# A four-layer graph network on one core: the first transposed adjacency made on TensorE, two of four turn transfers issued by ScalarE, and the last element's third layer in plain products

## The chip, the cores and the metric

The kernel runs on one core of one Trainium2 chip. The metric is device time in microseconds (us), as the median of several executions of the whole program. One more execution is recorded by the profiler; its trace and its page are what this document reads. The profiled execution has a time of its own, which stands in the table below beside its span (first to last instruction).

## What is computed

There are 32 independent batch elements. Each has 512 nodes of 128 features (`x`) and a dense 512x512 matrix `adj`. Four residual layers run one after the other on each element; every layer first normalizes its rows and applies ReLU. Cut to what matters:

```python
h = relu(layernorm(x)); A1 = adj + I; r = rowsum(A1) ** -0.5
x = x + leaky_relu((A1 * r[:, None] * r[None, :]) @ (h @ W) + b)               # layer 0

h = relu(layernorm(x))
i, o, n = (elu(h @ Wk.T + bk) for Wk, bk in (in, out, node))
x = x + tanh(concat([adj @ i, n, adj.T @ o]) @ W_upd.T + b_upd)                # layer 1

f = relu(layernorm(x)); R = adj / rownorm(adj); C = adj / colnorm(adj)
for k in range(4):       # inputs of 128, 128, 256, 384 features: earlier f are appended
    f = tanh(concat([R @ (f @ ws + bs), f @ wn + bn, C.T @ (f @ wd + bd)]) @ wu + bu)
x = x + f                                                                      # layer 2

h = relu(layernorm(x)); m = tanh(adj @ (h @ W_msg.T + b_msg))
x = x + GRU(m, h)                                                              # layer 3
```

All of it is float32.

## The kernel before, in words

**Tiles.** A node dimension of 512 is cut into `NC = 4` chunks of 128 partitions. An element holds `a` (its `adj`, 1 MB) and `aT` (the transposed `adj`), each as 128 x 4 x 512 in SBUF. Layer 3 loads the transposed matrix a second time (`aT2`), since layer 2 has changed `aT` in place.

**Products.** TensorE works in two halves of 64 output rows: `by_halves` issues one matmul for each half, and the two run side by side. In this document a *pair* is such a product on both halves. Each of its two matmuls leaves two records in the trace, so a pair is four records.

**Layer 2 with fewer products.** `features` (steps 1, 3 and 4 of layer 2) and `edges` (step 2) do the products with the two matrices in a scheme of seven products of half size instead of eight. It needs sums of blocks: `made_of` makes them of `aT` and `a` on VectorE (four operations of 128x512 for each matrix), `left_sums` makes them of the features, and the results are put together by more additions on VectorE (`p`, `de`, `to`, line 792).

**Turns.** Features are needed both with nodes on partitions and with features on partitions. For elements 2 to 30, `turned` does the change: VectorE transposes 32x32 blocks into `blk` (line 698), four DMAs write `blk` to DRAM (`away`, line 707: `turn_turned<-blk`), and one DMA reads it back (line 711: `turned<-turn_turned`). All five are issued by SyncE (SP), which issues nearly all DMAs. An element has seven turns (three in `transposed`, one in `second`, three in `added_rows`), 203 in all. Elements 0, 1 and 31 (`at_ends`) turn on TensorE instead (`turn_on_pe`: a product with the identity).

**Order.** `Plan` collects every operation of all 32 elements as an `Op` with an engine, an estimated duration, what it reads and writes, and a key: the element's due time (`PERIOD`) less the longest way from the operation to the element's end, plus a hand-set shift by the name of the result (`LATER`). `order` then plays the engines forward with these estimates, takes the ready operation of the lowest key on each engine, gives it its buffers (`places`: 27 of 2 KB, 7 of 4 KB and so on, and the 8 banks of PSUM), and so fixes the order of each engine's instructions. On the chip each engine goes through its list in that order. Loads of later elements are held back while a turn is under way (`yields`, `way`). The loads in `FIRST` go out ahead of everything else, in the order of that list. `kept_warm` puts products of no use (`ps_idle<-ident`) on TensorE wherever the plan has it idle for longer than its constant `SHORT`.

**Start.** Element 0 is on its own: `x0`, `a0` and `aT0` are loaded in pieces of 256 KB, `normed_by_chunk` sums the rows of each piece of `a` on VectorE and takes a power on GpSimd, the diagonal blocks of `aT` get the identity added (`diag`, line 1023), and the first aggregation `psh` (lines 1024 to 1031) runs through `aT` column chunk by column chunk. Then come `lin` (line 1038) and the rest of layer 0, beside the folding of the weights (`fold`, `foldb`, in `setup`), which reads `raw0`, `raw2` and `raw3`.

**End.** Element 31 has nobody behind it: its last layer is `gates_turned`, whose parts are worked off in halves.

Of the kernel before, what the change touches and what calls it, by code (L numbers as in the profile page):

```python
# [14 lines left out]
AF = mybir.ActivationFunctionType  # L15
# [3 lines left out]
P = 128  # L19
# [6 lines left out]
ENDING = -5.5  # L26
LATER = {"de": 4, "nb": 4, "rows": 1, "ps_a2": -4, "f3": -4, "s34": 2, "n": 4, "sd": -10, "w": 2, "st2": -8, "f4": 2, "blk": 1, "rep": 1, "s12": 4, "ps_second": -1, "hn": -2, "f2p": 4, "f2": 2, "ps_gate": -1}
SMALL = 8

FIRST = ["x0", "a0", "aT0", "c", "raw0", "w1", "r1", "raw2", "raw3", "x1", "a1", "aT1", "x2", "a2", "aT2"]  # L30

# [260 lines left out]
def gnn_stack(  # L292
# [15 lines left out]
    dram = ctx.enter_context(tc.tile_pool(name="dram", bufs=1, space=bass.MemoryType.DRAM))  # L308
    plan = Plan(sb, psum, {"bank": 8, "s2": 27, "s4": 7, "s6": 4, "s8": 8}, {"bank": 0, "s2": 2, "s4": 0, "s6": 0, "s8": 0})

# [161 lines left out]
    def program(b):  # L472
# [144 lines left out]
        def load(dst, src, kb, rank, behind=()):  # L617

            name = f"{rank}{b}"
            rank, kb = first(name), kb * (2 if name == "a0" else 1)  # L620

            n = NC // pieces
            for k in range(pieces):
                s = slice(k * n, (k + 1) * n)
                op("SP", 0.4, lambda s=s: nc.sync.dma_start(dst.ap()[:, s, :], src[:, s, :]),
                   [], [(dst, set(range(NC)[s]))], kb=kb / pieces, rank=rank, yields=rank is None, behind=behind)

        op("SP", 0.4, lambda: nc.sync.dma_start(xt.ap(), x[b]), [], [xt], kb=256, rank=first(f"x{b}"), yields=f"x{b}" not in FIRST)
        load(a, adj[b], 1024, "a")
        load(aT, adjt[b], 1024, "aT")  # L630

# [62 lines left out]
        def turned(m, name, quiet=False):  # L694
# [8 lines left out]

            def away(k):
                if bounce.tile is None:
                    bounce.tile = dram.tile([P, NC, P], F32, name=bounce.name, tag=f"{bounce.kind}_{bounce.slot}", bufs=1)
                nc.sync.dma_start(bounce.tile[:, k, :].rearrange("(b s) n -> s b n", b=NC), blk.ap()[k * P // NC:(k + 1) * P // NC])  # L707

            for k in range(NC):
                op("SP", 0.4, lambda k=k: away(k), [blk], [(bounce, {k})], kb=64)  # L710
            back = op("SP", 0.4, lambda: nc.sync.dma_start(mT.ap(), bounce.tile), [bounce], [mT], kb=256)
# [130 lines left out]
        def features(i, sd, nodes, made, f_new):  # L842

            st = buf("s4", (P, 4, NC, Q), "st")
            left_sums(H, lambda h, k: lambda: sd.ap().rearrange("p (q k) (o h f) -> p q k o h f", k=2, o=2, h=2)[:, :, k, :, h, :],
# [60 lines left out]
        def edges(f1r, made, ge):  # L908


            st = buf("s2", (P, 4, 2, Q), "st2")
# [109 lines left out]
        else:  # L1021
            for k in range(NC):
                op("DVE", t_tt(P), lambda k=k: nc.vector.tensor_tensor(diag.ap()[:, k:k + 1, :], *own(k, 1), op=ALU.add), [(aT, {k}), ID], [(diag, {k})])
        psh = plan.bank("agg")
        for c in range(NC if b == 0 else 0):
            for lo, hi in ((0, c * P), (c * P, (c + 1) * P), ((c + 1) * P, N)):
                if lo == hi:
                    continue
                mm(psh, lambda t, lo=lo, hi=hi: t[:, lo:hi], lambda c=c: hr.ap()[:, c, :],
                   (lambda c=c: diag.ap()[:, c, :]) if lo == c * P else (lambda c=c, lo=lo, hi=hi: aT.ap()[:, c, lo:hi]),  # L1030
                   hi - lo, c == 0 and lo == 0, c == NC - 1 and hi == N, [(hr, {c}), (diag if lo == c * P else aT, {c})])
        if b:
# [87 lines left out]

        made = [made_of(m) for m in (aT, a)]
        for i, (wsd, wn) in enumerate(W_L2):
# [100 lines left out]
```

## Time and profile before

| | |
|---|---|
| median of 4 runs | 2253.42 us (2250.16 to 2254.67) |
| the profiled execution | 2251.52 us |
| its span | 2249.7 us |
| TensorE (PE) busy | 2231.9 us, 99% |
| VectorE (DVE) busy | 1762.9 us, 78% |
| ScalarE (ACT) busy | 1219.0 us, 54% |
| GpSimd (POOL) busy | 230.9 us, 10% |
| DMA | 264.43 MB, mean 118 GB/s |
| granted TensorE clock | 1.0 over the whole span |

Between the profiled time and the span lie 1.8 us, and the median lies 1.9 us above the profiled time. "Busy" counts an instruction from its start to its end; matmuls overlap, so a busy TensorE can still have small holes. The products of no use count as busy too. SPq and ACTq are the instruction queues of SP and ScalarE when they issue DMAs. L838 and L364 are the lines of the two helpers that issue nearly all products, L792 the one that issues VectorE's sums, so groups are told apart by their tiles.

### The profile page before, as it was taken

Reading aid. Unit: us, or ns where it says so; the run is one execution under the profiler, and the core shown is the slowest. Engines: PE = TensorE matmul, PEld = TensorE weight load, DVE = VectorE, ACT = ScalarE, POOL = GpSimd, SP = SyncE. Lnnn points to the kernel's source line nnn. Section 1 sums busy time; section 2 is a strip of 40 time slices with the busy share of each in tenths; the row PEclk is TensorE's granted clock in tenths of the full one; section 3 lists DMA queues with packets and bytes.
Section 4 is the critical chain, followed back from the end, with each engine's and each line's share of the span. In section 5 each row is a group of like instructions: output and inputs, shape, how many; then the busy total and the mean of one; then the engine's idle time right before and its main releaser. Section 6 shows DMA issues by size and latency. Waiting matters only on the chain.

```text
span 2249.7 us, 47725 instructions
## 1 busy us (share of the span) xinstructions
PE 2231.9 (99%) x18332; PEld 1437.7 (64%) x18332; DVE 1762.9 (78%) x4657; ACT 1219.0 (54%) x2793; POOL 230.9 (10%) x203
## 2 busy tenths in 40 slices
PE   9999999999999999999999999999999999999999
PEld 6665566676556656775567755666666655655576
DVE  7776878888778788788788787887787887787754
ACT  8654565654556545556545556545565455564323
POOL 2110111100111101111001111011111011110000
PEclk9999999999999999999999999999999999999999
DMA  7131434344344444344443344443444443433211
GB/s 257 39 103 42 140 109 128 118 138 133 107 126 129 123 132 122 107 126 118 140 132 112 121 127 122 136 124 109 133 124 127 136 120 109 128 106 114 76 53 57
DMA packets 199139, 264.43 MB, mean 118 GB/s; under 512 B 25984, under 2 KB 130688, under 8 KB 198912
## 3 DMA queue, kind: packets, MB, share of 16 engines
q1 hardware_dynamic: 198624, 261.26, 38.2%
q8 instruction: 144, 2.36, 0.4%
q14 instruction: 83, 0.68, 0.1%
q10 hardware_dynamic: 288, 0.13, 0.0%
HBM read 199.18 MB, written 62.13 MB: 116 GB/s over the span
## 4 chain that ended last, share of the span: by engine, by line
PE 84%; DVE 6%; DMA 5%; SPq 2%; ACT 1%; issue 1%; POOL 0%; POOLq 0%; DVEq 0%; ACTq 0%
PE ps_pa L838 17%; PE ps_agg L364 16%; PE ps_cd L838 16%; PE ps_sd L364 10%; PE ps_seven L364 4%; PE ps_pb L838 3%; DMA turned<-turn_turned 3%; PE ps_b L838 3%; PE ps_gate L364 2%; PE ps_upd L364 2%; PE ps_second L364 2%; PE ps_a L838 2%; SPq L707 2%; PE ps_c L838 1%; PE ps_msg L364 1%; DMA turn_turned<-blk 1%
## 5 line engine op out<-in xcount | busy, mean ns | idle before, releaser
L838 PE MATMUL ps_pb<-made,st 128*64 128x256 f32 x1536 | 392.8, 379 | 0.0
L677 POOL TENSOR_TENSOR sc<-v,neg_half 128x4 f32<-128x4 f32 x127 | 171.3, 1349 | 1762.6 <-DVE v L638 1717.8
L364 PE MATMUL ps_sd<-w_sb,f 128*64 128x256 f32 x2048 | 267.4, 379 | 0.5 <-ACT f L1127 0.4
L838 PE MATMUL ps_pa<-aT,sd 128*64 128x256 f32 x768 | 227.9, 379 | 0.0
L838 PE MATMUL ps_cd<-aT,st 128*64 128x256 f32 x768 | 223.1, 380 | 2.3 <-DVE st L792 2.0
L838 PE MATMUL ps_cd<-a,st 128*64 128x256 f32 x768 | 223.8, 379 | 0.0
L838 PE MATMUL ps_pa<-a,sd 128*64 128x256 f32 x768 | 223.7, 379 | 0.0
L838 PEld LDWEIGHTS ps_pb<-made,st 128*64 128x64 f32 x1536 | 209.4, 137 | 0.8 <-DVE p L792 0.4
L364 PEld LDWEIGHTS ps_sd<-w_sb,f 128*64 128x64 f32 x2048 | 163.1, 137 | 69.0 <-issue 18.4
L838 PE MATMUL ps_pb<-made,sd 128*64 128x256 f32 x768 | 197.0, 379 | 0.0
L901 ACT ACTIVATE f<-to,cf_sb 64x512 f32<-64x512 f32 x192 | 117.5, 612 | 125.5 <-DVE to L792 121.0
L689 ACT ACTIVATE h<-xr,nb,sc 128x128 f32<-128x128 f32 x384 | 158.0, 484 | 25.0 <-DVE nb L685 24.6
L778 DVE TENSOR_TENSOR sd<-ps_sd,rf_sb 128x512 f32<-128x512 f32 x192 | 123.1, 683 | 45.7 <-PE ps_sd L364 45.6
L838 PEld LDWEIGHTS ps_pa<-aT,sd 128*64 128x64 f32 x768 | 105.1, 137 | 65.3 <-issue 25.3
L792 DVE TENSOR_TENSOR p<-p,ps_pb 64x256 f32<-64x256 f32 x192 | 81.4, 424 | 64.8 <-PE ps_pb L838 41.9
L838 PEld LDWEIGHTS ps_pa<-a,sd 128*64 128x64 f32 x768 | 105.1, 137 | 41.1 <-issue 2.2
L364 PE MATMUL ps_agg<-a,rep 128*64 128x512 f32 x512 | 128.2, 592 | 0.0
L364 PE MATMUL ps_agg<-aT,msg 128*64 128x512 f32 (+1 forms) x528 | 126.6, 579 | 0.0
L792 DVE TENSOR_TENSOR to<-p,ps_pb 64x256 f32<-64x256 f32 x96 | 40.8, 425 | 107.1 <-PE ps_pb L838 105.9
L838 PEld LDWEIGHTS ps_cd<-aT,st 128*64 128x64 f32 x768 | 102.4, 137 | 34.2 <-issue 4.6
L364 PE MATMUL ps_agg<-aT,rep 128*64 128x512 f32 x512 | 122.9, 592 | 0.1
L838 PEld LDWEIGHTS ps_cd<-a,st 128*64 128x64 f32 x768 | 104.4, 137 | 27.9 <-issue 1.1
(224 smaller groups left out, 5828.9 us busy)
## 6 DMA issues: line engine op xcount, KB each, us to landing
aT<-in_adjt SPq DMA_DIRECT2D x124, 512.0 KB, 6.1
turn_turned<-blk SPq DMA_DIRECT2D x696, 64.0 KB, 1.8
turned<-turn_turned SPq DMA_DIRECT2D x174, 256.0 KB, 2.8
a<-in_adj SPq DMA_DIRECT2D x62, 512.0 KB, 7.3
rows<-bounce SPq DMA_DIRECT2D x32, 512.0 KB, 4.1
shares<-bounce SPq DMA_DIRECT2D x32, 512.0 KB, 3.7
x<-in_x SPq DMA_DIRECT2D x32, 256.0 KB, 4.5
out<-xr SPq DMA_DIRECT2D x31, 256.0 KB, 2.7
```

The lines of the kernel that those rows point to most:

```text
L364: nc.tensor.matmul(to[c], weight[:, c], data, start=start, stop=stop, skip_group_check=True)
L677: op("POOL", t_pow(n), lambda: nc.gpsimd.tensor_tensor(inv.ap()[:, :n], v8.ap()[:, :n], neg_half[:, :n], op=ALU.pow), [v8, NH], [(inv, {0})])
L689: op("ACT", t_act(D, 2), lambda c=c: nc.scalar.activation(h.ap()[:, c, :], xin.ap()[:, c, :], AF.Relu, bias=nb.ap()[:, c:c + 1], scale=inv ...
L707: nc.sync.dma_start(bounce.tile[:, k, :].rearrange("(b s) n -> s b n", b=NC), blk.ap()[k * P // NC:(k + 1) * P // NC])
L778: op("DVE", t_tt(N), lambda ps=ps, h=h: nc.vector.tensor_add(sd.ap()[:, 2 * h:2 * h + 2, :], ps.ap().rearrange("p (j v) -> p j v", j=2), a ...
L792: return op(engine, us, lambda: eng.tensor_tensor(o(), x(), y(), op=ALU.subtract if sign < 0 else ALU.add), reads, writes)
L838: nc.tensor.matmul(to(), lhs(), rhs(), start=start, stop=True, skip_group_check=True)
L901: op("ACT", t_act(n, 1), lambda: nc.scalar.activation(f_new.ap()[rows, cols], src(), AF.Tanh, bias=cf_sb[rows, i:i + 1]), reads + [(CF, {i ...
```

## The change

Six edits, made together:

1. **First transpose.** `aT0` is no longer loaded. TensorE turns each of the four row chunks of `a0` into a bank of PSUM (16 pairs of 128 columns), ScalarE copies each bank into `aT`, and `diag` is added out of PSUM. The first aggregation goes by rows of `a` instead of columns: block by block as the row chunks come.
2. **Turns.** The second and fourth of the four transfers of a turn (`k % 2`) are issued by ScalarE (`nc.scalar.dma_start`) as an operation in ScalarE's list. The read back stays with SP.
3. **Last element.** With `PLAIN = 1` element 31 makes no block sums: `features` and `edges` take plain products of 512 columns, gathered in one bank (`made is None`).
4. **Buffers.** 29 places of 2 KB instead of 27 (and 3 kept free for older elements instead of 2), 6 of 4 KB instead of 7.
5. **Keys.** `LATER` has six more names.
6. **Estimate of a load.** The plan takes the load of `a0` as 1.2 times its size and not 2 times.

The diff, cut to its core:

```diff
-LATER = {"de": 4, ..., "f2": 2, "ps_gate": -1}
+PLAIN = 1
+LATER = {"de": 4, ..., "f2": 2, "ps_gate": -1, "node": -8, "y": 8, "made": -1, "f1r": 4, "turn_turned": -1, "ge": 4}
...
-FIRST = ["x0", "a0", "aT0", "c", "raw0", "w1", "r1", "raw2", "raw3", "x1", "a1", "aT1", "x2", "a2", "aT2"]
+FIRST = ["x0", "a0", "c", "raw0", "w1", "r1", "raw2", "raw3", "x1", "a1", "aT1", "x2", "a2", "aT2"]
...
-    plan = Plan(sb, psum, {"bank": 8, "s2": 27, "s4": 7, "s6": 4, "s8": 8}, {"bank": 0, "s2": 2, "s4": 0, "s6": 0, "s8": 0})
+    plan = Plan(sb, psum, {"bank": 8, "s2": 29, "s4": 6, "s6": 4, "s8": 8}, {"bank": 0, "s2": 3, "s4": 0, "s6": 0, "s8": 0})
...
-            rank, kb = first(name), kb * (2 if name == "a0" else 1)
+            rank, kb = first(name), kb * (1.2 if name == "a0" else 1)
...
-        load(aT, adjt[b], 1024, "aT")
+        if b:
+            load(aT, adjt[b], 1024, "aT")
+        else:
+            turned_rows = [plan.bank(f"turn_{r}") for r in range(NC)]
+            for r, ps in enumerate(turned_rows):
+                for c in range(NC):
+                    turn_on_pe(ps, c, lambda r=r, c=c: a.ap()[:, r, c * P:(c + 1) * P], [(a, {r})])
+                op("ACT", t_act(N), lambda r=r, ps=ps: nc.scalar.copy(
+                    aT.ap()[:, :, r * P:(r + 1) * P], ps.ap().rearrange("p (c n) -> p c n", c=NC)), [ps], [(aT, {0, 1, 2, 3, NC + r})])
...
-            def away(k):
+            def away(k, queue=nc.sync):
...
             for k in range(NC):
-                op("SP", 0.4, lambda k=k: away(k), [blk], [(bounce, {k})], kb=64)
+                if k % 2:
+                    op("ACT", plan.ISSUE, lambda k=k: away(k, nc.scalar), [blk], [(bounce, {k})]).land = plan.TRANSFER + 64 / plan.ALONE - plan.ISSUE
+                else:
+                    op("SP", 0.4, lambda k=k: away(k), [blk], [(bounce, {k})], kb=64)
...
+            if made is None:                                                    # in features
+                ps = plan.bank("agg")
+                for n, (data, reads) in enumerate(nodes):
+                    mm(ps, lambda t: t, lambda c=NODES[i][n]: wt(c), data, N, n == 0, False, [reads(0), reads(1), (W2F, {i})])
+                for c in range(NC):
+                    for o, m in enumerate((aT, a)):
+                        mm(ps, lambda t: t, lambda c=c, o=o: sd.ap()[:, c, o * D:(o + 1) * D], lambda c=c, m=m: m.ap()[:, c, :], N,
+                           False, c == NC - 1 and o == 1, [(sd, {2 * c + o}), (m, {c})])
+                return op("ACT", t_act(N, 1), lambda: nc.scalar.activation(f_new.ap(), ps.ap(), AF.Tanh, bias=cf_sb[:, i:i + 1]), [ps, (CF, {i})], [f_new])
...
+            if made is None:                                                    # in edges
+                for h in range(2):
+                    ps = plan.bank("agg")
+                    for c in range(NC):
+                        def emit(ps=ps, h=h, c=c):
+                            lhs = f1r.ap() if len(f1r.shape) == 2 else f1r.ap().rearrange("p c d -> p (c d)")
+                            for o, m in enumerate((aT, a)):
+                                nc.tensor.matmul(ps.ap()[HALVES[o], :], lhs[:, c * P + h * Q:c * P + (h + 1) * Q], m.ap()[:, c, :],
+                                                 start=c == 0, stop=c == NC - 1, skip_group_check=True)
+                        op("PE", t_mm(N), emit, [f1r, (aT, {c}), (a, {c})], [ps])
+                    op("ACT", t_act(N), lambda ps=ps, h=h: nc.scalar.copy(ge.ap()[:, h, :], ps.ap()), [ps], [(ge, {h, h + 2})])
+                return
...
-                op("DVE", t_tt(P), lambda k=k: nc.vector.tensor_tensor(diag.ap()[:, k:k + 1, :], *own(k, 1), op=ALU.add), [(aT, {k}), ID], [(diag, {k})])
+                op("DVE", t_tt(P), lambda k=k: nc.vector.tensor_tensor(diag.ap()[:, k, :], turned_rows[k].ap()[:, k * P:(k + 1) * P], ident, op=ALU.add), [(turned_rows[k], {k}), ID], [(diag, {k})])
...
-        made = [made_of(m) for m in (aT, a)]
+        made = None if b >= B - PLAIN else [made_of(m) for m in (aT, a)]
```

## The prediction

> **What bounds it now.** First the page, then TensorE's waits, then the chain of waits, then the two ends by the timeline.
>
> ```profile
> PE 2231.9 (99%) x18332; PEld 1437.7 (64%) x18332; DVE 1762.9 (78%) x4657; ACT 1219.0 (54%) x2793; POOL 230.9 (10%) x203
> ...
> PE 84%; DVE 6%; DMA 5%; SPq 2%; ACT 1%; issue 1%; POOL 0%; POOLq 0%; DVEq 0%; ACTq 0%
> ```
>
> TensorE works nearly always and carries 84% of the chain. So the time is its work, plus what it loses before, between and behind that work. Next, its waits:
>
> ```profile
> PE ps_msg L364 <- ACT hT L745: 7.3, 14, 1.2
> PE ps_cd L838 <- DVE st L792: 2.0, 4, 0.6
> ...
> PE ps_second L364 <- DVE ge L792: 0.8, 2, 0.5
> ```
>
> In the steady stretch only one wait has weight: `msg` waits for the end of a turn, 7.3 us in 14 of 29 elements. A wait also empties the pipeline. A matmul is seen for 0.17 us longer than the next one needs to start (0.38 us against 1.73 us for eight of 64x256 side by side), so 14 waits cost up to 2.4 us more.
>
> Does the work explain the rest? An inner element has 25 pairs of 512 columns, 103 of 256 and 8 of 128. In runs without a wait, one pair takes 0.8585, 0.4315 and 0.2185 us: 67.7 us. The chain has the same step at 356.50 and, 23 elements later, at 1929.36: 68.4 us for each. So 0.7 us of an element is loss, some 20 us over 29 elements; the waits above are half of that.
>
> A turn, from SP's timeline (start, time taken), and ScalarE's only two DMA issues:
>
> ```profile
> 2214.07 1.78 SPq L707 DMA_DIRECT2D turn_turned<-blk  x4
> 2217.25 0.34 SPq L711 DMA_DIRECT2D turned<-turn_turned  x1
> ...
> 0.73 0.41 ACTq L393 DMA_DIRECT2D w_sb<-in_w  x1
> 1.17 0.46 ACTq L394 DMA_DIRECT2D r_sb<-in_brow  x1
> ```
>
> Four issues take 1.78 us one behind the other, the read back goes out 3.18 us after the first, and `hT` is copied at 2220.80: 6.7 us a turn. The start, on TensorE:
>
> ```profile
> 1.39 8.48 PE L364 MATMUL ps_idle<-ident 128*64 128x128 f32 x108 [1.39 <-POOL ident masks.py:199]
> 9.99 0.44 PE L364 MATMUL ps_agg<-diag,h 128*64 128x128 f32 x4
> ...
> 15.37 1.09 PE L364 MATMUL ps_lin<-w_sb,agg 128*64 128x128 f32 x16 [0.16 <-PE ps_idle L364]
> ...
> 30.92 2.79 PE L364 MATMUL ps_agg<-aT,rep 128*64 128x512 f32 x12
> ...
> 46.50 2.35 PE L364 MATMUL ps_idle<-ident 128*64 128x128 f32 x40
> ```
>
> Nothing real runs before 9.99; useless products come again until 51.03, where the steady stretch begins.
>
> **The sum, part by part,** against the profiled 2251.52 us. The order of instructions of both kernels gives the counts.
>
> *Work.* First transpose: 16 pairs x 0.2185 = 3.5 us more. Last element: 42 more pairs of 512 and 76 fewer of 256, 36.06 - 32.79 = 3.3 us more. Useless pairs: 57 for 98. Block sums (VectorE, eight operations at 0.69 us) and `left_sums` go with the last element; nobody waits for them except at the end.
>
> *Start to `lin`* (15.37 us now). Without 1.05 MB of `aT0`, what follows `a0` in the queue lands some 2.6 to 3.2 us earlier (at the 408 and 325 GB/s of the windows around 10 us). `a0`'s pieces land as now: the second at 5.85, the third shortly before VectorE takes it at 7.90, so the fourth near 8.5. From there the reduction (0.68), two small operations, the power (0.54), two more and `h` (0.49) take some 2.5 us with their signals; now the product of the scales waits from 11.09 to 12.27 behind operations that need `aT` and `c`. Turning, copying (0.58) and `diag` of the last piece lie beside that. The aggregation could end near 11.7 and `lin` start at 12.6. But the new order puts `fold0`, `foldb0` and `foldb2` ahead of `lin`, and `foldb2` reads `raw2`: 1.1 MB behind `raw0`, which landed at 14.65 and now would near 11.6, so `raw2` lands at 13.4 to 14.3. With 0.75 us of folds, `lin` starts at 14.2 to 15.0. I take **-0.8**; bounds 0 and -2.8.
>
> *From `lin` to layer 1's aggregation* (15.5 us): a chain through VectorE, ScalarE and GpSimd, the same in both. 0 (bounds +-0.5).
>
> *On to the steady stretch.* Now 16 useless pairs cost 0.86 + 2.51 + 0.86 us between 44.72 and 51.03. The new order fills that place with the aggregation of element 2 and has 2, 4 and 4 useless pairs later on: 2.2 us. **-2.0**; bounds -4 and 0.
>
> *Steady.* A turn's issues become two and two, so the last goes out about 0.9 us earlier. ScalarE gets 406 issues: 14 an element, at 0.41 to 0.46 us up to 6.4 us of 68.4. It was 55% busy there and becomes 64%. An issue that waits for `blk` holds all that stands behind it in ScalarE's list: `h`, `rep`, `f`, `hT`, for which TensorE waits in turn. The row shows two issues at the start and nothing in steady work, so the price is open: 0 if the issue slips into waits (ScalarE waits 125 us for `ps_pa` alone), 0.46 an element if one of fourteen reaches TensorE: 13.3 us. The gain is bounded by the `msg` waits, 9.7 us. But the plan knows the shorter turn and moves `msg` up with it, and what it doesn't know stays: the read back took up to 4.75 us in the chain against a median of 2.8. I take a fifth of the gain and no price, the row of ScalarE's own waits being nearest: **-2**; bounds -9.7 and +13.3.
>
> The Trainium skill ("DMA: Bandwidth & Descriptors", section "Issuing engines are not separate DMA queues") speaks against more: transfers from several engines share the same 16 DMA engines, and only the time of issuing is saved. By it a turn gains the 0.9 us and its landing (1.8 us) nothing; if landing were halved as well, a turn would gain 1.8. The trace can't tell, since no turn is split yet.
>
> *End.* From the last product of element 30's layer 2 (about 2197.3) to `msg` at 2221.47 runs a chain with two turns: 24.2 us, while TensorE has 22.7 us to do, some 6 of it useless. Two turns at -0.9 give 22.4; the new order has 21.5 us of TensorE work there, so the chain still decides. Useless pairs from there on and shortly before fall from 36 to 21 (-3.3), which pays for the plain products (+3.3). Against the shorter chain stands that the order leaves 26.1 us of work from `msg` on, where it was 23.3. **-1.1**; bounds -3 and +2. The last 20 us (turn, gates, output) are the same chain in both.
>
> *Buffers and keys* show in the order alone; their worth lies in the steady bounds.
>
> Sum: -0.8 - 2.0 - 2 - 1.1 = **-5.9**: 2245.6 profiled, and with the 1.9 us by which the median lies higher **2247.5 us**. Its own range is 2243.5 to 2250.
>
> **Rivals.**
>
> *TensorE no longer waits for turns.* All 9.7 us go instead of 2: 2239.8. For it: the waits are short (at most 1.2 us) and 0.9 comes off each turn. Against: the plan moves up too.
>
> *ScalarE comes late.* Place: the two issues in ScalarE's list of each turn, with `h` or `rep` behind them. Price 13.3 us as above: 2253.42 - 3.9 + 13.3 = 2262.8. It decides once TensorE loses over 0.13 us an element (3.9/29) and shows as slower from 0.29. For it: ScalarE is in order, and the two issues stand where VectorE may be late. Against: it idles 45%, and its issues took no longer than SP's.
>
> *The change does not do what it says at the ends.* `raw2` holds `lin` at 15.4, and the end's extra work eats its chain: only the filled hole is left, 2253.42 - 2 = 2251.4.
>
> *A cold TensorE.* In the first microseconds products run slowly, with 1.00 granted all the while:
>
> ```profile
> 2.00:4.00 2.00, 2.00 (x22) 2.00 (x20) 0.33 (x2) 0.28 (x1) 0.00 (x0) 1.00 0.97 316
> ...
> 6.00:8.00 2.00, 2.00 (x38) 2.00 (x36) 1.01 (x5) 0.49 (x1) 1.21 (x3) 1.00 0.92 301
> ```
>
> These are windows of 2 us; the first number in brackets counts TensorE's records: 22, later 38. The changed kernel has 6 useless pairs and then turns that wait for pieces of `a0`. If it stays at 0.36 us a pair, the last four turns and the aggregation take some 3 us longer, `lin` starts at 15.6 and the -0.8 becomes +0.2: 2248.5. The Trainium skill ("TensorE: Matmul & The Clock Gate", section "What's actually happening") says just this: half clock until a window of some 3.4 us was busy. It agrees with the two rows.
>
> **From cases to numbers.** Forecast 0.45, no waits 0.22, late ScalarE 0.20, nothing at the ends 0.08, cold 0.05. About 0.2% (4.5 us) is what a measurement of this kernel can tell from no change, so faster means under 2248.9: three quarters of the forecast's range, all of "no waits", half of "cold": 0.58. Slower needs most of ScalarE's price: 0.20. The rest, 0.22, is the same. The range takes in most of both steady bounds: 2238 to 2260, leaving out the far parts of "no waits" and of "late ScalarE".
>
> **What would show it.** Right: `lin` starting between 14 and 15; no useless products between 44 and 51; the read back issued some 2.3 us after a turn's first issue; `msg` waits of 4 to 7 us in all; 23 steady elements at 68.3 us. Wrong: a steady step off 68.4 by over 0.15 us either way, waits of TensorE for `rep`, `h` or `f` behind ScalarE's issues, or issues on ScalarE far over 0.46 us.

## The result, and the profile after

The changed kernel takes 2248.1 us (median of 42 runs, 2244.42 to 2251.69), the kernel before 2252.57 us (60 runs, 2248.31 to 2258.17). The ratio is 0.9979, 95% interval 0.9975 to 0.9984: 4.5 us faster. The profiled execution took 2250.35 us with a span of 2248.6, against 2251.52 and 2249.7 before. So the two profiles lie only 1.2 us apart: that of before is 1.0 us under its median, that of after 2.3 us over its own. What is known of that comes below.

The page of the changed kernel, the busy times and the chain of waits:

```profile
PE 2229.1 (99%) x18108; PEld 1491.7 (66%) x18108; DVE 1739.4 (77%) x4610; ACT 1225.7 (55%) x2788; POOL 214.1 (10%) x203
...
PE 76%; DVE 12%; DMA 6%; ACT 2%; issue 1%; ACTq 1%; SPq 0%; POOL 0%; DVEq 0%; POOLq 0%
```

TensorE is as full as before. VectorE has taken 6 points of the chain, SyncE's queue has left it. TensorE's waits (line waited for, us in total, times, longest):

```profile
PE ps_msg L365 <- ACT hT L757: 3.1, 7, 0.8
PE ps_agg L365 <- DVE rep L1100: 2.9, 4, 2.0
PE ps_cd L850 <- DVE v L647: 2.8, 6, 1.2
```

The wait for the end of a turn fell from 7.3 to 3.1 us. The waits ahead of `ps_cd` did not fall: 2.0 us for `st` before, 2.8 us for `v` now. New are a wait of 2.0 us in one piece for `rep`, and two waits of the first transpose (1.03 and 0.46 us in the timeline of the start below). The timeline of a turn, first SyncE's queue, then ScalarE's:

```profile
405.28 0.79 SPq L716 DMA_DIRECT2D turn_turned<-blk  x2
408.00 0.34 SPq L723 DMA_DIRECT2D turned<-turn_turned  x1
```

```profile
405.29 0.84 ACTq L716 DMA_DIRECT2D turn_turned<-blk  x2
```

Two and two issues run side by side, and the read back goes out 2.72 us after the first of them. Over all 203 turns the median of that distance fell from 3.27 to 2.67 us.

The steady step, by the start of `msg` in elements 4 and 27, in TensorE's timeline before and after:

```profile
427.63 0.66 PE L364 MATMUL ps_msg<-w_sb,hT 128*64 128x128 f32 x8 [0.21 <-ACT hT L745]
...
2001.19 0.66 PE L364 MATMUL ps_msg<-w_sb,hT 128*64 128x128 f32 x8 [0.23 <-ACT hT L745]
```

```profile
434.19 0.61 PE L365 MATMUL ps_msg<-w_sb,hT 128*64 128x128 f32 x8
...
2001.34 0.64 PE L365 MATMUL ps_msg<-w_sb,hT 128*64 128x128 f32 x8
```

Before, 23 elements take 1573.56 us, 68.42 each; after, 1567.15 us, 68.14 each. But element 4 comes 6.6 us later than before: the steady stretch wins, and most of the win pays for a worse start. TensorE's timeline there:

```profile
5.25 1.55 PE L365 MATMUL ps_turn<-ident,a 128*64 128x128 f32 x12 [1.03 <-DMA a<-in_adj]
7.26 4.55 PE L365 MATMUL ps_turn<-ident,a 128*64 128x128 f32 x52 [0.46 <-DVE diag L1058]
...
13.22 0.82 PE L365 MATMUL ps_agg<-diag,h 128*64 128x128 f32 x8 [0.32 <-ACT h L671]
...
18.89 1.04 PE L365 MATMUL ps_lin<-w_sb,agg 128*64 128x128 f32 x16
...
33.79 4.49 PE L365 MATMUL ps_agg<-aT,rep 128*64 128x512 f32 x12 [1.96 <-DVE rep L1100]
...
44.95 1.92 PE L365 MATMUL ps_agg<-aT,h 128*64 128x512 f32 x8
```

The first aggregation starts at 13.22 (9.99 before), `lin` at 18.89 (15.37 before). Thirteen pairs of the first transpose (52 records) take 4.55 us, 0.35 us a pair where 0.2185 is the full pace. The layer-1 aggregation comes at 33.79 (30.92 before) and takes 4.49 us where it took 2.79. The last line is the filled hole: element 2's aggregation stands where useless products stood from 44.7 to 51. Two windows show where the slow products end (us, busy time and records of PE, PEld, DVE, ACT, POOL, granted clock, DMA share, GB/s):

```profile
8.00:10.00 2.00, 2.00 (x22) 2.00 (x20) 1.24 (x4) 1.45 (x3) 2.00 (x4) 1.00 1.01 408
10.00:12.00 2.00, 2.00 (x38) 2.00 (x36) 0.75 (x5) 0.88 (x2) 1.07 (x3) 1.00 0.89 270
```

TensorE does 22 records in the first and 38 in the second. The trace's first record of the granted clock begins at 10.35 us, with 1.00; ahead of it there is none, and a row without a record prints 1.00 as well. So "the clock came up at 10.35 us" means here that this record begins there, and the pace of the products agrees with it. In the kernel before the first record begins at 6.28 us.

ScalarE's timeline (first the table load of the kernel before, then the changed kernel) and VectorE's show two more reasons:

```profile
3.72 1.28 ACT L662 ACT_TABLE_LOAD   x1 [3.72 <-DMA x<-in_x]
```

```profile
7.29 1.28 ACT L638 ACT_TABLE_LOAD   x1 [7.29 <-DVE diag L1058]
8.58 0.58 ACT L638 COPY aT<-ps_turn 128x512 f32<-128x512 f32 x1
...
12.19 0.58 ACT L638 COPY aT<-ps_turn 128x512 f32<-128x512 f32 x1 [0.62 <-DVE diag L1058]
```

```profile
10.32 0.29 DVE L1058 TENSOR_TENSOR diag<-ps_turn,ident 128x128 f32<-128x128 f32 x1 [1.09 <-ACT aT L638]
```

ScalarE's table load (1.28 us) stands directly ahead of its first operation, and that is now a copy of `aT` which waits for data; before, it lay at 3.72, and ScalarE's first `h` after it still waited 2.08 us for VectorE. And `diag`, which reads the same PSUM bank as the copy, is placed behind it, so VectorE stands for 1.09 us, with the small operations for `h` queued behind.

Where the time went, as sums of TensorE's work from the trace (pairs at 0.8585, 0.4315 and 0.2185 us; "loss" is the rest of the stretch; two of the experiments below are added):

| us | before | after | `aT` loaded | closed gaps |
|---|---|---|---|---|
| 0–100: real work | 78.3 | 76.0 | 77.7 | 78.1 |
| first transpose / useless pairs | 0 / 13.5 | 3.5 / 7.0 | 0 / 13.5 | 3.5 / 10.1 |
| loss | 8.2 | 13.5 | 8.7 | 8.3 |
| 100–2100: real work / loss | 1978.9 / 21.0 | 1982.5 / 16.6 | 1982.6 / 16.5 | 1984.2 / 15.0 |
| from 2100: length | 149.7 | 148.6 | 145.1 | 145.1 |

At 100 us the changed kernel is 2.3 us of work behind; by 2100 it is 3.6 us better than that, 1.3 us ahead. (Real work and loss between 100 and 2100 us leave out 0.9 us of useless pairs in the last three columns.)

### The profile page after: what moved, and what is told of

Read it like the earlier page. It is cut to its first block, busy times and chain, and to the rows that moved or that the text cites. A ratio compares the mean times of both kernels' runs of the same rounds, so it can differ in the third digit from the quotient of the medians.

```text
span 2248.6 us, 47332 instructions
## 1 busy us (share of the span) xinstructions
PE 2229.1 (99%) x18108; PEld 1491.7 (66%) x18108; DVE 1739.4 (77%) x4610; ACT 1225.7 (55%) x2788; POOL 214.1 (10%) x203
## 4 chain that ended last, share of the span: by engine, by line
PE 76%; DVE 12%; DMA 6%; ACT 2%; issue 1%; ACTq 1%; SPq 0%; POOL 0%; DVEq 0%; POOLq 0%
PE ps_agg L365 15%; PE ps_pa L850 14%; PE ps_cd L850 13%; PE ps_sd L365 9%; PE ps_pb L850 4%; PE ps_seven L365 4%; DMA turned<-turn_turned 3%; PE ps_gate L365 3%; PE ps_second L365 2%; PE ps_b L850 2%; PE ps_upd L365 2%; DMA turn_turned<-blk 2%; PE ps_a L850 2%; PE ps_c L850 2%; DVE blk L707 1%
## 5 line engine op out<-in xcount | busy, mean ns | idle before, releaser
L850 PE MATMUL ps_pb<-made,st 128*64 128x256 f32 x1488 | 387.8, 379 | 0.0
L686 POOL TENSOR_TENSOR sc<-v,neg_half 128x4 f32<-128x4 f32 (+1 forms) x127 | 154.2, 1215 | 1691.6 <-DVE v L647 1484.1
L850 PE MATMUL ps_cd<-aT,st 128*64 128x256 f32 x744 | 214.9, 380 | 3.5 <-DVE v L647 2.8
L850 PE MATMUL ps_pa<-aT,sd 128*64 128x256 f32 x744 | 216.3, 379 | 0.0
L365 PEld LDWEIGHTS ps_sd<-w_sb,f 128*64 128x64 f32 x2048 | 172.8, 137 | 63.8 <-issue 20.6
L850 PE MATMUL ps_cd<-a,st 128*64 128x256 f32 x744 | 211.5, 379 | 0.0
L850 PEld LDWEIGHTS ps_pb<-made,st 128*64 128x64 f32 x1488 | 200.9, 137 | 4.6 <-DVE p L804 0.9
L922 ACT ACTIVATE f<-to,cf_sb 64x512 f32<-64x512 f32 (+1 forms) x186 | 113.7, 612 | 142.3 <-DVE to L804 141.5
L850 PE MATMUL ps_pb<-made,sd 128*64 128x256 f32 x744 | 191.2, 379 | 0.1
L365 PE MATMUL ps_agg<-aT,h 128*64 128x512 f32 (+2 forms) x532 | 122.2, 573 | 0.0
```

The source lines that it names most:

```text
L365: nc.tensor.matmul(to[c], weight[:, c], data, start=start, stop=stop, skip_group_check=True)
L686: op("POOL", t_pow(n), lambda: nc.gpsimd.tensor_tensor(inv.ap()[:, :n], v8.ap()[:, :n], neg_half[:, :n], op=ALU.pow), [v8, NH], [(inv, {0})])
L850: nc.tensor.matmul(to(), lhs(), rhs(), start=start, stop=True, skip_group_check=True)
L922: op("ACT", t_act(n, 1), lambda: nc.scalar.activation(f_new.ap()[rows, cols], src(), AF.Tanh, bias=cf_sb[rows, i:i + 1]), reads + [(CF, {i ...
```

## The experiments

Each ratio is against the kernel before on the same chip, with its 95% interval; an amount in us is the ratio's difference times 2252.6. Three chips were used, on which the kernel before has medians of 2251.86, 2254.27 and 2256.08 us; so kernels are compared by their ratios, and the measured times alone do not compare from one experiment to the next. The order of instructions is computed from the kernel's own model, so an edit moves instructions everywhere, unless the text says that the order was kept.

**1. The first transpose undone.** `aT` of element 0 is loaded. With it the plan's estimate for `a0` (edit 6), the making of `diag` and the order of the first aggregation go back to those of the kernel before; the rest is the changed kernel.

```diff
-FIRST = ["x0", "a0", "c", "raw0", ...
+FIRST = ["x0", "a0", "aT0", "c", "raw0", ...
...
-            rank, kb = first(name), kb * (1.2 if name == "a0" else 1)
+            rank, kb = first(name), kb * (2 if name == "a0" else 1)
...
-        if b:
-            load(aT, adjt[b], 1024, "aT")
-        else:
-            turned_rows = ...
+        load(aT, adjt[b], 1024, "aT")
```

> The changed kernel with the first transpose undone: `aT` of element 0 is loaded again, everything else stays. TensorE's list then has 2213.1 us of pairs (87 of them useless) against 2210.0 us in the changed kernel (57 useless). Theory A (the turns on TensorE make the start slow: late table load, shared bank, cold clock): `lin` starts near 15.4 again instead of 18.9, the layer-1 aggregation near 31 instead of 33.8 with no fall of the clock before it, and the time falls by 2 to 4 us to 2244 to 2246 (ratio to before 0.9962 to 0.9971). Rival B (a late start is made good later, TensorE's list is what counts): no gain or a loss of up to 3 us, 2248 to 2251 (0.998 to 0.9995).

Measured: 2246.39 us, ratio 0.9973 (0.9961 to 0.9984). TensorE's timeline:

```profile
15.09 1.09 PE L365 MATMUL ps_lin<-w_sb,agg 128*64 128x128 f32 x16 [0.16 <-PE ps_idle L365]
...
30.63 2.79 PE L365 MATMUL ps_agg<-aT,rep 128*64 128x512 f32 x12
```

`lin` and the layer-1 aggregation are back where they were, the latter at full pace (2.79 us for twelve records). The ratio lies just outside theory A's range, 1.4 us under the changed kernel, and the intervals overlap. The work sums of the two profiles say more: 4.8 us less loss before 100 us against 3.1 us more pairs in TensorE's list. But 1.7 us of that is the clock that fell in this one execution of the changed kernel (4.49 against 2.79 us for the layer-1 aggregation), and 1.7 of the 3.5 us between the two spans lie behind 2100 us (a loss of 6.6 against 8.3 us), where the edit changes nothing but the order. That the first transpose does not pay is likely, then, and not shown.

**2. All transfers on SyncE, order worked out anew.**

```diff
-                if k % 2:
-                    op("ACT", plan.ISSUE, lambda k=k: away(k, nc.scalar), ...
-                else:
-                    op("SP", 0.4, lambda k=k: away(k), ...
+                op("SP", 0.4, lambda k=k: away(k), ...
```

> The changed kernel with all four transfers of a turn issued by SyncE again, and the order worked out anew for that. Theory A (the two queues make a turn 0.6 us shorter, and that is the steady stretch's gain of some 4 us): turns take 3.2 to 3.3 us from first issue to the issue of the read back, and the time rises by 3 to 5 us to 2251 to 2253 (ratio 0.9995 to 1.000). Rival B (the keys and the buffers made the steady gain, the issues nothing): it stays within 1 us of 2248.1 (0.9975 to 0.9984). TensorE's list is 2 us shorter than in the changed kernel (48 useless pairs for 57), which by itself would bring it to 2246 at best.

Measured: 2253.61 us, ratio 1.0005 (0.9997 to 1.0014), 5.9 us above the changed kernel. Theory A, just above its range. Turns take 3.26 us to the read back, and the step from element 4 to 27 is 68.46 us.

**3. All transfers on SyncE, the order kept.**

```diff
-                    op("ACT", plan.ISSUE, lambda k=k: away(k, nc.scalar), ...
+                    op("ACT", plan.ISSUE, lambda k=k: away(k), ...
```

> The changed kernel with its order of instructions on TensorE, VectorE, GpSimd and ScalarE kept as it is; only the two transfers that ScalarE issued are issued by SyncE instead, at the place that the order gives them. It shows what the split of the issues is worth when nothing else moves. Theory A: each turn's read back goes out 0.6 us later than the order is made for, TensorE's waits for the ends of turns (`msg` on `hT`) grow from 3.1 to 8 to 14 us, and the time rises to 2253 to 2259 (ratio 1.000 to 1.003). Rival B (transfers share the same engines, the issue is not what a turn waits for): within 2 us of 2248.1. Rival C (issues on ScalarE cost ScalarE's followers more than the turn gains): faster than 2248.1.

Measured: 2290.97 us, ratio 1.0171 (1.0157 to 1.0185), 43 us above the changed kernel. TensorE's waits:

```profile
PE ps_msg L365 <- ACT hT L757: 33.2, 28, 2.1
```

The direction is theory A's, the size is far over it: nearly every element waits for its turn, 1.2 us on average, and the step grows to 69.4 us. The turns were only 0.65 us longer in the median (0.85 in the mean). It looks as if the order leaves hardly any room between a turn's planned end and its use, so that a delay reaches TensorE; this was not followed turn by turn. In three of the four runs the mean granted clock was 0.997 to 0.998, and the one at 1.000 was the fastest (2287.25 us), so some 4 of the 43 us go with a falling clock. Beside experiment 2 this shows how much an order made for a slower turn recovers: all but 6 of 43 us.

**4. Two transfers on ScalarE in the kernel before, nothing else.**

```diff
-                op("SP", 0.4, lambda k=k: away(k), ...
+                if k % 2:
+                    op("ACT", plan.ISSUE, lambda k=k: away(k, nc.scalar), ...
+                else:
+                    op("SP", 0.4, lambda k=k: away(k), ...
```

> The kernel before with one edit: two of the four transfers of a turn are issued by ScalarE, and the order is worked out for that with the keys and buffers of before. TensorE's list is the same in length as before (2212.2 us). Theory A (the issues are most of the steady gain): the 20.9 us that TensorE loses between 100 and 2100 us fall to 16 to 18, the time falls by 2 to 4 us, ratio 0.998 to 0.999. Rival B (keys and buffers made the gain): within 1 us of before, 0.9996 to 1.0004. Rival C (the keys of before do not fit the shorter turns): slower than before, above 1.0004.

Measured: 2261.52 us, ratio 1.0039 (1.0025 to 1.0052). Rival C: the part of the change that should gain loses 9 us alone. TensorE waits 12.0 us, 25 times, for `st` of VectorE; turns are as short as in the changed kernel (2.72 us).

**5. The changed kernel with the keys and buffers of before.**

```diff
-LATER = {..., "ps_gate": -1, "node": -8, "y": 8, "made": -1, "f1r": 4, "turn_turned": -1, "ge": 4}
+LATER = {..., "ps_gate": -1}
-    plan = Plan(sb, psum, {"bank": 8, "s2": 29, "s4": 6, ...}, {"bank": 0, "s2": 3, ...})
+    plan = Plan(sb, psum, {"bank": 8, "s2": 27, "s4": 7, ...}, {"bank": 0, "s2": 2, ...})
```

> The changed kernel with the keys and the numbers of buffers of the kernel before, the order worked out anew. The run that put ScalarE's issues alone into the kernel before came out 9 us slower with TensorE waiting 12 us for `st` of VectorE, so theory A (the shorter turns need the new keys): the same waits come back, 2254 to 2260, ratio 1.001 to 1.0035. Rival B (that slowness came from the last element or the first transpose of the kernel before, which this kernel does not have): within 2 us of 2248.1.

Measured: 2266.95 us, ratio 1.0053 (1.0039 to 1.0067). Theory A, above its range. The waits, and one of them in TensorE's and VectorE's timelines:

```profile
PE ps_cd L850 <- DVE st L804: 12.2, 25, 1.4
```

```profile
572.43 0.40 PE L850 MATMUL ps_cd<-aT,st 128*64 128x256 f32 x1 [1.30 <-DVE st L804]
```

```profile
568.55 0.69 DVE L738 TENSOR_TENSOR xr<-turned,xr 128x512 f32<-128x512 f32 x1 [1.50 <-DMA turned<-turn_turned]
...
571.86 0.76 DVE L804 TENSOR_TENSOR st<-sd 128x256 f32<-128x256 f32 x2
```

VectorE works its list in order. It stands for 1.50 us before `xr`, which needs a turn's result, and `xr`, its moments, `sd` and `st` follow; TensorE waits for `st`. In the changed kernel the same place has a shorter wait and an earlier `st`. TensorE is nearly as far in both (its last `sd` products start at 570.51 here and at 570.11 there), and in the changed kernel it has `msg` to do ahead of `ps_cd`:

```profile
567.39 0.69 DVE L738 TENSOR_TENSOR xr<-turned,xr 128x512 f32<-128x512 f32 x1 [1.03 <-DMA turned<-turn_turned]
...
570.40 0.40 DVE L804 TENSOR_TENSOR st<-sd 128x256 f32<-128x256 f32 x1
```

This is one place, read from the trace. That all 25 waits have this form was not followed.

**6. Both halves old:** SyncE alone, old keys and buffers, the edits of experiments 2 and 5 together.

```diff
-LATER = {..., "node": -8, "y": 8, ...}
+LATER = {..., "ps_gate": -1}
...
-                if k % 2:
-                    op("ACT", plan.ISSUE, ...
```

> The changed kernel with all transfers on SyncE and with the keys and buffers of the kernel before: what is left of the change are the first transpose on TensorE and the plain products of the last element. It is the fourth corner beside: both new 0.9979, new keys with SyncE alone 1.0005, old keys with ScalarE 1.0053. Theory A (keys and split issues only pay together; the first transpose costs some 2 us and the plain products gain some 2 to 3): 2250.5 to 2253.5, ratio 0.999 to 1.0005, far below what adding the two separate losses would mean. Rival B (old keys are worse in themselves): 1.002 or more.

Measured: 2257.37 us, ratio 1.0004 (0.9995 to 1.0013). Theory A, by the ratio. The four corners, all with the first transpose and the plain products:

| ratio | keys and buffers of before | new keys and buffers |
|---|---|---|
| SyncE alone | 1.0004 | 1.0005 |
| two on ScalarE | 1.0053 | 0.9979 |

The new keys and buffers alone are worth nothing, the split issues alone cost 11 us, both together gain 5.6 us. The parts of the change do not simply add up either: the first transpose and the plain products together come to +0.9 us in this corner (0.9995 to 1.0013), where experiments 1 and 8, in the order of the changed kernel, put them at 1.4 us lost and 2.9 us gained.

**7. New keys, old buffers.**

```diff
-    plan = Plan(sb, psum, {"bank": 8, "s2": 29, "s4": 6, ...}, {"bank": 0, "s2": 3, ...})
+    plan = Plan(sb, psum, {"bank": 8, "s2": 27, "s4": 7, ...}, {"bank": 0, "s2": 2, ...})
```

> The changed kernel with the numbers of buffers of the kernel before (27 of 256 KB, 7 of 512 KB, 2 kept per element instead of 29, 6 and 3) and the new keys. The run with old keys and old buffers came out 17 us slower, with 25 waits of TensorE for `st` of VectorE. Theory A (the keys did that): within 3 us of the changed kernel, ratio 0.9975 to 0.999, and hardly a wait for `st`. Rival B (the buffers did it): ratio 1.003 or more, with the waits for `st`.

Measured: 2244.31 us (5 runs, 2243.72 to 2248.55), ratio 0.9955 (0.9943 to 0.9968), faster than theory A's range, and without a wait for `st`: with the new keys and the split issues the waits are gone with either numbers of buffers, and with these keys the old buffers are better than the new ones. New buffers with old keys were not run. By its ratio this version beats both kernels, and its interval lies apart from that of the changed kernel. Why is open. TensorE's list is only 0.9 us shorter (2209.2 against 2210.0 us), the steady step is the same (68.18 us), and the profiled execution was the slowest of the five, 1.8 us under the changed kernel's. Between these two profiles the gain lies behind 2100 us (146.8 us long against 148.6).

**8. The plain products undone.**

```diff
-PLAIN = 1
+PLAIN = 0
```

> The changed kernel with the last element's layer 2 computed as in all others (block sums instead of plain products), the order worked out anew. TensorE's list is as long as in the changed kernel (2210.06 against 2210.04 us: 3.3 us less of real pairs, 15 more useless ones). Theory A (the end came out even, as the two traces' 4.8 and 4.6 us of loss say): 2247 to 2249, ratio 0.9975 to 0.9985. Rival B (without the block sums VectorE is free earlier and the end's chain is shorter): slower by 1 to 3 us, 2249 to 2251.

Measured: 2252.76 us, ratio 0.9992 (0.9983 to 1.0000). Rival B, at its far edge: the last element without block sums is worth 2.9 us by the ratios, 1.7 us between the two profiled spans. The interval still touches that of the changed kernel. Until 2100 us both kernels run alike; the difference is at the end (150.3 us behind 2100 us against 148.6).

**9. Two repairs of the start:** an early table load, and `diag` made from `aT` in SBUF.

```diff
-        op("POOL", 0.2, lambda: nc.gpsimd.memset(neg_half, -0.5), [], [NH])
+        def halves():
+            nc.gpsimd.memset(neg_half, -0.5)
+            nc.scalar.copy(scratch, neg_half[:, :1])
+        op("POOL", 0.2, halves, [], [NH])
...
-... diag.ap()[:, k, :], turned_rows[k].ap()[:, k * P:(k + 1) * P], ident, op=ALU.add), [(turned_rows[k], {k}), ID], ...
+... diag.ap()[:, k, :], aT.ap()[:, k, k * P:(k + 1) * P], ident, op=ALU.add), [(aT, {NC + k}), ID], ...
```

> The changed kernel with two repairs at its start: a copy of one column at the very beginning brings ScalarE's table load there (ahead of the data), and the four `diag` blocks are made from `aT` in SBUF instead of from the PSUM banks that TensorE still fills. Theory A (late table load and shared banks delay the start): the copies of `aT` start near 7 instead of 8.58, the first aggregation near 11 instead of 13.22, `lin` at 14.5 to 16.5 instead of 18.89, loss before 100 us falls from 12.1 to 8 to 10, time 2244.5 to 2246.5 (ratio 0.9964 to 0.9973). Rival B (the cold clock is what counts, 0.35 us a pair): turns end near 11 as before, `lin` above 17, time within 1 us of 2248.1.

Measured: 2252.97 us, ratio 0.9993 (0.9984 to 1.0002). Rival B has the start right (the turns end at 11.07 us and `lin` lies above 17), but the time is outside both ranges. TensorE's timeline:

```profile
5.38 5.69 PE L366 MATMUL ps_turn<-ident,a 128*64 128x128 f32 x64 [1.19 <-DMA a<-in_adj]
...
17.23 1.04 PE L366 MATMUL ps_lin<-w_sb,agg 128*64 128x128 f32 x16
```

`lin` comes 1.7 us earlier. But the turns are as slow as before (0.36 us a pair), and the new order loses some 7.4 us between 200 and 400 us, where the changed kernel loses 3.0. The edit was small, but its dependencies changed the order far behind it. So the next repairs kept the order.

**10. The gaps closed with useless pairs, the order kept:** 3 pairs ahead of the first turn, 2 ahead of the fourth, 9 ahead of the layer-1 aggregation on `rep`.

```diff
+MORE = {("ps_turn_0_0", 1): 3, ("ps_turn_0_0", 4): 2, "rep_0": 9}
...
+            n = more.pop(self.mark(o), 0)
+            if n:
+                used = {x.slot for x in banks if x.since < o.ready and x.until > o.ready - 0.1}
+                out.append((next(k for k in range(self.places["bank"]) if k not in used), n))
             out.append(o)
```

> The changed kernel with 14 more useless pairs and nothing else: 3 ahead of the first turn, 2 ahead of the fourth, 9 ahead of the layer-1 aggregation of element 0, so that TensorE has no gap there. Theory A (the clock is a cause of its own): 1.00 is granted from about 6.3 instead of 10.35 us, the thirteen turns take 2.9 instead of 4.55 us, the clock does not fall again after 34 us, in any execution; time 2245 to 2247 (ratio 0.9966 to 0.9975). Rival B (copies and `diag` pace the start, a faster TensorE only waits more): the start stays, `lin` at 18 to 19; only the second fall of the clock goes, which is half of 2.1 us: 2247. Rival C: useless pairs delay real ones, 2249 or more.

Measured: 2247.18 us, ratio 0.9969 (0.9958 to 0.9981), 2.2 us under the changed kernel for 3.1 us of extra useless work; the intervals overlap. The timeline:

```profile
7.87 3.06 PE L384 MATMUL ps_turn<-ident,a 128*64 128x128 f32 x52
...
18.08 1.04 PE L384 MATMUL ps_lin<-w_sb,agg 128*64 128x128 f32 x16
...
33.40 2.79 PE L384 MATMUL ps_agg<-aT,rep 128*64 128x512 f32 x12
```

The turns run at full pace, yet `lin` gains only 0.8 us, since the copies start at 9.19, behind the table load: that much of rival B holds. Another 1.7 us come from the layer-1 aggregation, which takes 2.79 instead of 4.49 us. Windows of the changed kernel (us, busy time and records of PE, PEld, DVE, ACT, POOL, granted clock, DMA share, GB/s):

```profile
34.00:36.00 2.00, 2.00 (x7) 0.64 (x5) 1.46 (x3) 2.00 (x6) 0.00 (x0) 0.56 0.95 375
36.00:37.60 1.60, 1.60 (x6) 0.54 (x4) 1.19 (x3) 1.60 (x6) 0.00 (x0) 0.50 1.04 417
```

and with the gaps closed:

```profile
34.00:36.00 2.00, 2.00 (x12) 0.60 (x10) 1.60 (x4) 2.00 (x6) 0.00 (x0) 1.00 0.99 389
```

The changed kernel waits 1.96 us for `rep` (31.83 to 33.79). From 34.24 on the granted clock is 0.50 for 3.41 us, and TensorE does 7 records in 2 us instead of 12. With nine useless pairs in that wait the clock stays at 1.00.

**11. The early table load alone, the order kept.** Here the copy stands behind ScalarE's two issues.

```diff
-        op("AQ", 0.5, lambda: nc.scalar.dma_start(
-            r_sb[:, :D], ...
+        def row_and_table():
+            nc.scalar.dma_start(r_sb[:, :D], ...
+            nc.scalar.copy(scratch, neg_half[:, :1])
+        op("AQ", 0.5, row_and_table, [], [(RS, {0})], kb=64)
```

> The changed kernel with one added instruction: ScalarE copies one column right behind its two DMA issues, so that its table load runs there; the order of everything else is the same as in the changed kernel. Theory A (the cold clock paces the turns: 13 pairs at 0.35 us, the last bank full near 11.8 us): the copies of `aT` start near 7.4, 9.1, 10.4 and 11.9 instead of 8.58, 9.71, 10.98 and 12.19, `h` and `lin` come at most 0.5 us earlier, the clock still falls in some executions, time 2247.5 to 2248.2. Rival B (the table load is the main delay): `lin` 1.3 us earlier, near 17.6, time near 2246.8.

Measured: 2250.09 us, ratio 0.9975 (0.9965 to 0.9984): 0.9 us better than the changed kernel, not separable from it. TensorE's timeline:

```profile
6.59 3.06 PE L366 MATMUL ps_turn<-ident,a 128*64 128x128 f32 x52 [0.46 <-DVE diag L1062]
...
16.73 1.04 PE L366 MATMUL ps_lin<-w_sb,agg 128*64 128x128 f32 x16
```

In this execution the turns ran at full pace without any help: the clock came up at 4.15 us, not at 10.35, with the same products ahead of it. So this profile can't separate the table load from the clock, and part of the 4.55 us above belongs to the one execution that was profiled. And though `lin` came 2.2 us earlier, the layer-1 aggregation came only 0.5 us earlier (33.31 us): `lin` is not all that it waits for.

**12. Both: gaps closed and early table load,** the order kept.

```diff
+MORE = {("ps_turn_0_0", 1): 3, ("ps_turn_0_0", 4): 2, "rep_0": 9}
...
+            nc.scalar.copy(scratch, neg_half[:, :1])
```

> The changed kernel with both: the 14 useless pairs that close TensorE's gaps at the start (2.2 us faster when they stood alone, ratio 0.9969) and the early table load. Theory A: with a warm TensorE the table load is the next bound, since the copies then started at 9.19 while the first bank was full at 7.9; `lin` moves from 18.08 to about 17, time 2246 to 2247, ratio 0.9963 to 0.9968. Rival B (the nine pairs ahead of the layer-1 aggregation are cut for a later start and now delay it): 2247 to 2248, as without the table load.

Measured: 2248.48 us, ratio 0.9968 (0.9956 to 0.9980), the same as without the table load. `lin` comes at 17.69 instead of 18.08, but the layer-1 aggregation only at 33.14 instead of 33.40. The traces bear out rival B's mechanism: VectorE ends the first part of `rep` at 32.59 us (32.84 in experiment 10), and the useless pairs run on until 33.08 (33.33). In the changed kernel the aggregation starts 0.14 us behind that part of `rep`, so the nine pairs hold it up by some 0.4 us in both. The ratio alone does not decide, as it lies at the edge of theory A's range. With the clock warm, these runs show no worth of the early table load.

## Why the prediction was right, and where it was not

It said 2247.5 and the kernel takes 2248.1, but that the number is so close is luck. In the profiles the parts come to -1.1 us (+2.3 for start and hole, -3.6 steady, +0.2 at the end) and not to -5.9. The median fits all the same, because the profiled execution of the changed kernel lies 2.3 us above its median, where the prediction took the profile to lie 1.9 us below.

Of the signs that it named for being right only one came, that no useless product is left between 44 and 51 us. `lin` came at 18.89 and not between 14 and 15, the read back 2.67 us after the first issue and not 2.3, the waits for `msg` are 3.1 us and not 4 to 7. The steady step of 68.14 us is 0.26 off 68.4, beyond the 0.15 that was named as a sign of being wrong. What held is the direction of the steady part and of the whole.

*Start to `lin`, -0.8:* wrong in sign. `lin` came 3.5 us later in the profiled execution. `raw2`, which I had made the bound, was not it: its fold ran at 16.9 to 18.9 behind a late aggregation. "Turning, copying and `diag` of the last piece lie beside that" is the step that failed. They are one chain through one bank after the other. Even in the execution with the clock up at 4.15 us and an early table load (experiment 11) `lin` came at 16.73, 1.4 us later than before. I had priced the copies at 0.58 us each, but neither the table load ahead of the first nor the order between copy and `diag`. The rival "a cold TensorE" (+0.2) named one of the mechanisms at a chance of 0.05 and missed that the copies, and not only the products, would be late. Its "with 1.00 granted all the while" misreads the row: between 2 and 4 us the trace has no record of the clock. That the clock falls once more behind the wait for `rep`, which cost 1.7 us, stands in no term.

*The hole, -2.0:* it was filled as said, with no useless pair between 44 and 51. What that is worth by itself no run shows. Start and hole together were to be 2.8 us ahead and are 2.3 us behind at 100 us: between 60 and 100 us the changed kernel has 1.3 us of useless pairs and 0.9 us of loss where the kernel before lost 0.2.

*Steady, -2:* the sign is right, the size too small. The profiles give -3.6 in work done between 100 and 2100 us, and 68.14 instead of the forecast 68.3 us a step. The turn gains 0.6 us, not 0.9. The Trainium skill ("DMA: Bandwidth & Descriptors", section "Issuing engines are not separate DMA queues") says that a second engine only saves time of issuing: the trace agrees, and shows less than that. The issues fell from 1.78 to 0.85 us, but from the end of the last issue to the read back it now takes 1.82 instead of 1.45 us. The step that was mis-sized is "I take a fifth of the gain": the waits for `msg` fell by 4.2 of 7.3 us. I had also left the keys and buffers in the bounds as if they were a detail. The corners show that they decide the sign.

*ScalarE's 406 issues at no price:* nothing in the changed kernel speaks against it. They took 0.36 us in the median (0.42 in the mean, 171 us in all), and where TensorE waits for ScalarE between 100 and 2100 us, the last operations of ScalarE hold no issue. (Its waits for VectorE were not followed back as far.) "ScalarE comes late" did not show, also not at the one place followed where the split lost time: there VectorE was late, behind a wait for a turn. The price by itself was not isolated.

*End, -1.1:* the profiles give +0.2. From 2100 us on the changed kernel had 1.3 us less to do (the 3.3 us of plain products left out) and took 1.1 us less. The plain products themselves are worth 1.7 to 2.9 us (experiment 8); what used that up in the new order was not found.

*From profile to median, +1.9:* with 60 runs the median of before lies 1.0 us above its profiled execution. The profile after lies 2.3 us above its median; that the clock fell in it is part of the reason. Of the 42 runs 21 have a mean clock of 0.999, with a median of 2249.0 us, and 21 have 1.000, with 2246.9. In all twelve runs with the gaps closed (experiments 10 and 12) it is 1.000.

## What to carry to other kernels

When an order of work is planned around a latency, the worth of a shorter latency is not a property of the edit: the same split issues cost 11 us with the old keys and buffers and gained 5.9 us with the new ones, and 43 us were lost when they were taken out of an order made for them. Test such an edit in all four corners, and repair a start with the order held fixed. The work that was moved to the first microseconds ran at 0.35 instead of 0.2185 us a pair in the profiled execution, behind a table load of 1.28 us, and bank by bank; count such a chain step by step before counting the bytes that it saves.

## What the runs showed of the hardware that was not expected

- The granted clock goes up and down on a grid of 3.41 us that does not start with the kernel: in the changed kernel it came up at 10.35 us and fell at 34.24, seven times 3.41 us later, for 3.41 us. With the same products at the start it came up at 10.35 us in this execution and at 4.15, 4.41 and 4.97 in others (experiments 11, 3 and 5). The Trainium skill ("TensorE: Matmul & The Clock Gate", section "What's actually happening") describes such a free-running window; the traces agree.
- A gap much shorter than that window is enough to bring the clock down. Gaps of about 1.96 us before `rep` did so in four profiled executions (the changed kernel, experiments 5, 7 and 8), gaps of 1.8 to 1.9 us did not in three others (2, 6 and 9). The Trainium skill ("TensorE: Matmul & The Clock Gate", section "Why this matters for your kernels") advises against gaps above some 3 us; here a gap of 1.96 us was enough. Two executions (3 and 11) had a gap of 1.96 us and no fall. In the changed kernel the gap lay wholly inside one window (30.83 to 34.24); in these two it lay across the border of two, by the grid worked out from the rise (borders at 31.72 and 31.46). So did the longest gap of experiment 4, 2.23 us (2080.84 to 2083.07, border at 2081.69), which brought no fall either.
- Engines that touch one PSUM bank were held one behind the other even where they touch different parts of it or both only read: TensorE's fourth turn waited 0.46 us for the first `diag` of VectorE, and later `diag` blocks waited up to 1.09 us for ScalarE's copies. In experiment 9, where VectorE read SBUF instead, the waits between TensorE's turns were gone. The trace shows these as waits for semaphores, which the program sets; a limit of the chip is not shown by them.
